# Sixteen-wavelength attention: part of the exponentials computed by exponent splitting and a polynomial on VectorE

## The chip, the cores and the metric

The kernel runs on one core of a Trainium2 chip. The time is device microseconds of that core for one execution of the whole program; lower is better. Engines are named as in the profile: PE (TensorE) does matmuls and transposes, ACT (ScalarE) activation functions, DVE (VectorE) elementwise work and reductions, POOL (GpSimd) a few elementwise operations, SP (SyncE) issues DMAs.

## The reference

Six layers act in turn on a residual stream of 4 batches x 1024 tokens x 128 features: a mixture of experts, a state-space layer, the same mixture again, a second mixture, an attention layer, and that second mixture again. Only the attention is touched by the change:

```python
# B = 4, S = 1024, H = 16 heads, D = 8, 16 wavelengths (WL)
Q, K, V = proj(Wq, bq), proj(Wk, bk), proj(Wv, bv)
def wl_step(acc, wl):
    cpm, iw = wl
    m = cpm[None, :, None, None]
    scores = jnp.einsum('bhqd,bhkd->bhqk', Q * m, K * m) * SCALE
    scores = scores * jnp.cos(KERR * scores * scores)
    attn = jax.nn.softmax(scores, axis=-1)
    return (acc + jnp.einsum('bhqk,bhkd->bhqd', attn, V) * iw, None)
```

KERR is 2.7e-12, so for the drawn data the cosine is 1 and the kernel takes a branch (`attention_small`) that leaves it out. What is left is, for each of 64 (batch, head) pairs and 16 wavelengths, a softmax of one 1024 x 1024 score matrix scaled by a number c(head, wavelength), times the values. One (batch, head, wavelength) is called a channel here: 1024 channels, each with a million exponentials, 8192 in each of the 128 partitions.

## The kernel before

The layers run one after the other with the residual stream `x_sb` resident in SBUF. In the attention, the scores of a (batch, head) `u` are computed once, less each row's maximum, into `xs[u]` (128 key rows x 8 key tiles x 1024 queries), and the 16 channels of `u` share them.

The loop over channels (lines 798 to 850) does this for each `wl` of each `u`:

- ACT computes `p_w = exp(c * xs[u])` over all 8192 elements in one instruction (line 812). `p_w` has two buffers.
- PE multiplies it by the values `vts` (lines 821 to 827): 8 key tiles `i` x 4 query quarters `r`, which show as 64 matmul records. The value tile carries a column of ones, so that the same product gives the softmax's denominator. The results lie in one of two PSUM tiles `ob`, in turn.
- DVE copies the product to SBUF (`os`, line 829), PE transposes it (line 842), and in every second channel DVE copies the transposes of two channels into `ot` (line 846).

Beside the channel of the current head, work for later ones is spread over the channels, a piece in each, by Python generators:

- `prepare(u + 2)`, 16 pieces: first `maxima`, in which PE computes a score tile (line 712), DVE reduces it to row maxima `nm` (line 726), and the eighth piece also transposes the maxima on PE (line 734) and writes them into a row of `qp` (line 741); then `head`, in which PE computes a score tile and DVE copies it to `xs` (line 750).
- `group`, in four channels of every fourth head: projections (line 691) and their copies with bias (line 698).
- `batch`, five pieces for each next batch: layer norm, transposes and values.
- `out`, eight pieces for each finished batch: `project` transposes the combined heads (line 511), copies them (`ct`, line 513), multiplies (line 515) and adds to `x_sb` (lines 517 and 518).
- `weigh`, once for each head, in the first channel of the next one: four DVE operations (lines 757 to 770) divide by the denominators, weight and sum the 16 wavelengths into `comb`.

For PE and DVE the order in the queues is the order in which the program is written: the whole loop stands under `manual_schedule(engines={PE, DVE})`. ACT runs its exponentials in order. An engine takes its instructions in order and each waits for the data that it needs, so an instruction that waits holds up all that stand behind it on its engine.

Within a channel of before, PE's queue has: the `o` matmuls, the side piece's matmuls, the score matmuls, the transposes of `os`. DVE's has: the `os` copy, `weigh` if due, the side piece, the score copy or reduction, the `ot` copy.

Of the kernel before, what the change touches and what calls it, by code (L numbers as in the profile page):

```python
# [19 lines left out]
F32 = mybir.dt.float32  # L20
I32 = mybir.dt.int32
AF = mybir.ActivationFunctionType
ALU = mybir.AluOpType
# [3 lines left out]
P = 128  # L27
B, L, C = 4, 1024, 128
GT = L // P
# [8 lines left out]
H, D, WL = 16, 8, 16  # L38
# [4 lines left out]
ROUND = 1.5 * 2.0**23  # L43
PI2_1 = 6.28125
PI2_2 = 0.0019350051879882812
PI2_3 = 2.0 * math.pi - PI2_1 - PI2_2
RSQRT = 1597463007.0
LN_TINY = -87.33654

# [23 lines left out]
def ln_stats(nc, sb, x, mv, rstd):  # L73

    n = x.shape[1]
    for i in range(n):
# [7 lines left out]
    nc.vector.tensor_scalar(  # L84
        rstd.bitcast(I32), a.bitcast(I32), -0.5, RSQRT, op0=ALU.mult, op1=ALU.add
    )
# [383 lines left out]
def half_sine(nc, sb, t, n):  # L470
# [6 lines left out]
    nc.vector.scalar_tensor_tensor(r, kk, -PI2_2, r, op0=ALU.mult, op1=ALU.add)  # L477
    nc.vector.scalar_tensor_tensor(r, kk, -PI2_3, r, op0=ALU.mult, op1=ALU.add)
    nc.vector.tensor_scalar(r, r, 4.0, -4.0, op0=ALU.min, op1=ALU.max)
# [42 lines left out]
NG = H // HG  # L522
QQ = 4
QW = L // QQ


def attention(tc, k):
# [8 lines left out]
    with ExitStack() as ctx:  # L536
# [51 lines left out]
        with tc.If(small > 0) as cmp:  # L588
            attention_small(tc, k, cc, iw)
# [4 lines left out]
def attention_small(tc, k, cc, iw):  # L594
# [9 lines left out]
    nc = tc.nc  # L604
    with (
# [9 lines left out]
        for x, w_t in (("q", k.wq), ("k", k.wk)):  # L615
# [11 lines left out]
            for j in range(HG):  # L627
                nc.sync.dma_start(
                    out=b_t[32 * j + 1 : 32 * j + 1 + D, :],
# [4 lines left out]
        vts = []  # L634
        for j in range(2):
            vt = one.tile([P, GT, H, D + 1], F32, name=f"vt{j}")
            nc.gpsimd.memset(vt[:, :, :, D : D + 1], 1.0)
            vts.append(vt)
        ob = []
        for j in range(2):  # L640
            o = ps_o.tile([P, 512], F32, name=f"o{j}", tag=f"o{j}")
            nc.vector.memset(o[:, 0:QW], 0.0)
            ob.append(o)

        xnt, qp, kp, comb, xs = {}, {}, {}, {}, {}

        def batch(b):

            xnt[b] = sb.tile([P, L], F32, name="xnt", bufs=1)
            mv = sb.tile([P, GT, 2], F32, name="mv")  # L650
            rstd = sb.tile([P, GT], F32, name="rstd")
            ln_stats(nc, sb, k.x_sb[:, ts(b, GT), :], mv, rstd)
            yield
            for half in range(2):
                pt = ps_t.tile([P, 4, P], F32, name="pt", tag="tr")
                for i in range(4):
                    t = b * GT + half * 4 + i
                    xn = sb.tile([P, C], F32, name="ln_xn", bufs=4)
                    nc.vector.tensor_scalar(
                        xn,  # L660
                        k.x_sb[:, t, :],
                        mv[:, half * 4 + i, 0:1],
                        rstd[:, half * 4 + i : half * 4 + i + 1],
                        op0=ALU.subtract,
                        op1=ALU.mult,
                    )
                    nc.tensor.transpose(pt[:, i, :], xn, k.ident)
                nc.vector.tensor_copy(xnt[b][:, ts(half, 512)], pt.rearrange("p a b -> p (a b)"))
                yield
            for half in range(2):  # L670
                pv = ps_t.tile([P, 4, H, D], F32, name="pv", tag="tr")
                for i in range(4):
                    nc.tensor.matmul(
                        pv[:, i], xnt[b][:, ts(half * 4 + i, P)], k.wv, start=True, stop=True
                    )
                for i in range(4):
                    nc.vector.tensor_tensor(
                        vts[b % 2][:, half * 4 + i, :, 0:D],
                        pv[:, i],
                        k.bv.rearrange("p (h d) -> p h d", d=D),  # L680
                        op=ALU.add,
                    )
                yield

# [61 lines left out]
        def head(u):  # L746
            n, j = divmod(u, HG)
            xs[u] = xp.tile([P, GT, L], F32, name="xs")
            for i in range(GT):
                nc.vector.tensor_copy(xs[u][:, i, :], score(j, kp[n], i, qp[n]))  # L750
                yield

        def weigh(u, ot):

            b, h = divmod(u, H)
            rz = sb.tile([P, WL, 2 * QQ], F32, name="rz", bufs=1)
            nc.vector.reciprocal(rz, ot[:, :, :, D])
            nc.vector.tensor_tensor(
                rz, rz, iw[:, :, None].to_broadcast([P, WL, 2 * QQ]), op=ALU.mult
            )  # L760
            nc.vector.tensor_tensor(
                ot[:, :, :, 0:D],
                ot[:, :, :, 0:D],
                rz[:, :, :, None].to_broadcast([P, WL, 2 * QQ, D]),
                op=ALU.mult,
            )

            if h == 0:
                comb[b] = sb.tile([P, 2, QQ, C], F32, name="comb")
            nc.vector.tensor_reduce(  # L770
                comb[b].rearrange("p c r e -> p (c r) e")[:, :, ts(h, D)],
                ot[:, :, :, 0:D].rearrange("p w t d -> p t d w"),
                AX.X,
                ALU.add,
            )

        def out(b):
            for c in range(2):
                for r in range(QQ):
                    project(nc, k, sb, ps_t, "tr", b * GT + 2 * r + c, comb[b][:, c, r, :])  # L780
                    yield

        def finish(*pieces):
            for piece in pieces:
                for _ in piece:
                    pass

        def prepare(u):

            yield from maxima(u)  # L790
            yield from head(u)

        n_heads = B * H
        with tc.manual_schedule(engines={mybir.EngineType.PE, mybir.EngineType.DVE}):
            finish(batch(0), group(0), prepare(0))
            ahead = prepare(1)
            next(ahead)
            for u in range(n_heads):
                n, j = divmod(u, HG)
                b, h = divmod(u, H)  # L800

                beside = []
                if j == 2 and n + 1 < B * NG:
                    beside.append((10, 14, group(n + 1)))
                if n % NG == 3 and j == 1 and b + 1 < B:
                    beside.append((4, 9, batch(b + 1)))
                if b > 0 and h == 2:
                    beside.append((2, 10, out(b - 1)))
                ot = sb.tile([P, WL, 2 * QQ, D + 1], F32, name="ot", bufs=1)
                for wl in range(WL):  # L810
                    p_w = xp.tile([P, GT, L], F32, name="p_w")
                    nc.scalar.activation(  # L812
                        p_w.rearrange("p a b -> p (a b)"),
                        xs[u].rearrange("p a b -> p (a b)"),
                        AF.Exp,
                        scale=cc[:, h, wl : wl + 1],
                    )
                    o = ob[wl % 2]
                    for i in range(GT):
                        for r in range(QQ):  # L820
                            nc.tensor.matmul(  # L821
                                o[32 * r : 32 * r + D + 1, 0:QW],
                                vts[b % 2][:, i, h, :],
                                p_w[:, i, ts(r, QW)],
                                start=(i == 0),
                                stop=(i == GT - 1),
                            )
                    os = sb.tile([P, QW], F32, name="os")
                    nc.vector.tensor_copy(os, o[:, 0:QW])  # L829
                    if u > 0 and wl == 0:  # L830
                        weigh(u - 1, last)
                    for lo, hi, piece in beside:
                        if lo <= wl < hi:
                            next(piece)
                    if wl == WL - 1 and u + 2 < n_heads:
                        finish(ahead)
                        ahead = prepare(u + 2)
                    next(ahead, None)
                    if wl % 2 == 0:
                        pt = ps_t.tile([P, 4, P], F32, name="pt", tag="tr")  # L840
                    for c in range(2):
                        nc.tensor.transpose(  # L842
                            pt[:, wl % 2 * 2 + c, :], os[:, ts(c, P)], k.ident
                        )
                    if wl % 2 == 1:
                        nc.vector.tensor_copy(
                            ot[:, wl - 1 : wl + 1].rearrange("p w t d -> p (w t) d"),
                            pt.rearrange("p a (r e) -> p (a r) e", e=32)[:, :, 0 : D + 1],
                        )
                last = ot  # L850
            weigh(n_heads - 1, last)
            finish(out(B - 1))

# [250 lines left out]
```

## Time and profile before

| | |
|---|---|
| median of 3 runs | 8823.45 us (8822.91 to 8829.49) |
| the profiled execution | 8833.98 us, its span in the trace 8832.1 us |
| before the attention loop's first exponential | 1424.5 us of the span |
| attention's channels | 7237.1 us of the span |
| after it | 170.5 us of the span |
| busy, whole span: PE, PEld, DVE, ACT, POOL | 7823.0, 3392.0, 3262.1, 7665.0, 608.7 us |
| granted PE clock, whole span | 0.918 |

PEld are weight loads, which run beside the matmuls. A busy PE is not a PE at its peak, as ends of matmuls are modelled. A mean duration of an instruction includes its latency, so that independent instructions in a row overlap a little: the distance from start to start is what counts in a chain. POOL's 608.7 us all lie ahead of the attention loop.

### The profile page before, as it was taken

The page shows a single profiled execution, that of the slowest core. Times are in us where ns is not written, and L with a number is a line of the kernel's source. Part 1 is how long each engine was busy: PE and PEld are TensorE (multiplying, and loading weights), DVE is VectorE, ACT ScalarE, POOL GpSimd, SP SyncE. Part 2 cuts the span into 40 slices and gives each one's busy share as a digit, 9 for nine tenths or more (in the row PEclk, how much of TensorE's full clock was granted, in tenths as well). Part 3 has the DMA queues.
Part 4 walks back from the last instruction along what each step waited for, and adds up shares of the span by engine and source line. Part 5 has one row for each costly group of instructions (what it writes and reads, how often), then busy time and mean ns, then how long its engine had stood idle before and what let it go on. Part 6 is the DMA issues. An engine that isn't in the chain of part 4 may idle for free. (4 is left out here: it accounts for less than half of the span.)

```text
span 8832.1 us, 164134 instructions
## 1 busy us (share of the span) xinstructions
PE 7823.0 (89%) x76474; PEld 3392.0 (38%) x76474; DVE 3262.1 (37%) x5409; ACT 7665.0 (87%) x1746; POOL 608.7 (7%) x579
## 2 busy tenths in 40 slices
PE   8888887999899998989999999999999999899985
PEld 5222253333333333333333333333333333333333
DVE  6777773323333333323233323223333333323222
ACT  3333325999999999999999999999999999999992
POOL 3444430000000000000000000000000000000000
PEclk9777787999999999999999999999999999999996
DMA  0000000000000000000000000000000000000000
GB/s 18 0 0 0 0 6 4 1 1 1 1 1 1 1 1 1 1 1 1 1 1 1 1 1 1 1 1 1 1 1 1 1 1 1 1 1 1 1 1 16
DMA packets 14326, 19.40 MB, mean 2 GB/s; under 512 B 2986, under 2 KB 12722, under 8 KB 13620
## 3 DMA queue, kind: packets, MB, share of 16 engines
q8 instruction: 609, 9.98, 0.5%
q1 hardware_dynamic: 9316, 6.01, 0.2%
q10 hardware_dynamic: 4304, 2.62, 0.1%
q14 instruction: 97, 0.79, 0.0%
HBM read 6.53 MB, written 2.10 MB: 1 GB/s over the span
## 5 line engine op out<-in xcount | busy, mean ns | idle before, releaser
L812 ACT ACTIVATE p_w<-xs,cc 128x8192 f32<-128x8192 f32 x1024 | 7188.6, 7109 | 48.5 <-DVE xs L750 29.1
L821 PE MATMUL o<-p_w,vt 128*9 128x256 f32 x65536 | 4055.1, 403 | 654.3 <-ACT p_w L812 653.4
L821 PEld LDWEIGHTS o<-p_w,vt 128*9 128x9 f32 x65536 | 1809.4, 95 | 2608.2 <-ACT p_w L812 804.3
L829 DVE COPY os<-o 128x256 f32<-128x256 f32 x1024 | 434.9, 425 | 3595.2 <-PE o L821 3595.2
L712 PE MATMUL s<-kp,qp 32*128 32x512 f32 x2048 | 1026.5, 621 | 0.0
L712 PE MATMUL s<-qp,kp 32*128 32x512 f32 x2048 | 1022.1, 619 | 0.0
L750 DVE COPY xs<-s 128x1024 f32<-128x1024 f32 x512 | 627.1, 1225 | 730.4 <-PE s L712 724.3
L726 DVE TENSOR_REDUCE nm<-s 128x1 f32<-128x1024 f32 x512 | 626.2, 1223 | 647.5 <-PE s L712 647.5
L712 PEld LDWEIGHTS s<-qp,kp 32*128 32x128 f32 x2048 | 343.6, 186 | 491.2 <-issue 486.9
L712 PEld LDWEIGHTS s<-kp,qp 32*128 32x128 f32 x2048 | 344.7, 186 | 471.7 <-issue 467.0
L842 PEld LDWEIGHTS pt<-ident,os 128*128 128x128 f32 x2048 | 206.2, 141 | 764.1 <-issue 669.0
L354 PE MATMUL yp<-hm,ident 128*128 128x512 f32 x512 | 388.7, 880 | 99.2 <-POOL hm L353 97.7
L842 PE MATMUL pt<-ident,os 128*128 128x128 f32 x2048 | 450.3, 302 | 19.6 <-DVE os L829 9.6
L336 ACT ACTIVATE da<-delta,neg_a 128x512 f32<-128x512 f32 x256 | 182.7, 721 | 291.9 <-DVE hst L342 291.5
L353 POOL TENSOR_TENSOR hm<-hst,c_sb 128x512 f32<-128x512 f32 x256 | 369.9, 1457 | 166.3 <-ACT c_sb L333 113.3
L178 ACT ACTIVATE r<-hp 128x512 f32<-128x512 f32 x160 | 95.5, 597 | 207.9 <-PE hp L176 185.5
L354 PEld LDWEIGHTS yp<-hm,ident 128*128 128x128 f32 x512 | 110.0, 252 | 348.9 <-POOL hm L353 318.0
L340 DVE TENSOR_TENSOR db<-du,bp 128x512 f32<-128x512 f32 x256 | 164.2, 682 | 152.9 <-PE bp L329 152.0
L333 ACT COPY c_sb<-cp 128x512 f32<-128x512 f32 x128 | 74.8, 585 | 166.1 <-PE cp L331 129.0
L342 DVE TENSOR_TENSOR_SCAN hst<-da,last,db 128x512 f32<-128x512 f32 x128 | 192.0, 1540 | 0.0
L180 POOL TENSOR_TENSOR h<-r 128x512 f32<-128x512 f32 x160 | 164.6, 1047 | 201.7 <-ACT r L178 201.3
L342 DVE TENSOR_TENSOR_SCAN hst<-da,db 128x512 f32<-128x512 f32 x128 | 171.1, 1372 | 5.6 <-POOL hm L353 4.4
(176 smaller groups left out, 3102.8 us busy)
## 6 DMA issues: line engine op xcount, KB each, us to landing
x_sb<-in_L_attn_x_dram ACTq DMA_DIRECT2D x4, 512.0 KB
c_w<-in_L_ffn_w_dram SPq DMA_DIRECT2D x4, 512.0 KB
out_dram<-x_sb SPq DMA_DIRECT2D x4, 512.0 KB
c_w<-in_L_ffn_w_stack_dram SPq DMA_DIRECT2D x1, 512.0 KB
c_w<-in_L_ffn_w_stack_dram ACTq DMA_DIRECT2D x1, 512.0 KB
c_ws<-in_L_ffn_ws_dram SPq DMA_DIRECT2D x2, 128.0 KB
c_w_in<-in_L_attn_W_in_dram SPq DMA_DIRECT2D x1, 256.0 KB
c_w_out<-in_L_attn_W_out_dram SPq DMA_DIRECT2D x1, 128.0 KB
```

Source lines behind the costliest of these rows:

```text
L180: nc.gpsimd.tensor_tensor(h, r, r, op=ALU.mult)
L336: nc.scalar.activation(da, delta[:, c, hc], AF.Exp, scale=neg_a[:, c, n : n + 1])
L342: nc.vector.tensor_tensor_scan(hst, da, db, 0.0 if half == 0 else last[:, c, n : n + 1], op0=ALU.mult, op1=ALU.add,)
L353: nc.gpsimd.tensor_tensor(hm, hst, c_sb, op=ALU.mult)
L354: nc.tensor.matmul(yp[c], k.ident, hm, start=(n == 0), stop=(n == NS - 1))
L712: nc.tensor.matmul(s[:, ts(half, 512)], a[row, ts(i, P)], c[row, ts(half, 512)], start=True, stop=True,)
L726: nc.vector.tensor_reduce(nm[:, i : i + 1], score(j, qp[n], i, kp[n]), AX.X, ALU.max, negate=True)
L750: nc.vector.tensor_copy(xs[u][:, i, :], score(j, kp[n], i, qp[n]))
L812: nc.scalar.activation(p_w.rearrange("p a b -> p (a b)"), xs[u].rearrange("p a b -> p (a b)"), AF.Exp, scale=cc[:, h, wl : wl + 1],)
L821: nc.tensor.matmul(o[32 * r : 32 * r + D + 1, 0:QW], vts[b % 2][:, i, h, :], p_w[:, i, ts(r, QW)], start=(i == 0), stop=(i == GT - 1),)
L829: nc.vector.tensor_copy(os, o[:, 0:QW])
L842: nc.tensor.transpose(pt[:, wl % 2 * 2 + c, :], os[:, ts(c, P)], k.ident)
```

## The change

512 of the 8192 exponentials of each channel (`SOFT = 512`: key tile 0 with the first 512 queries) are no longer computed by ACT. With log2(e) folded into the scale (`cc2`), DVE computes r = max(c x, -127), rounds it to a whole number p (adding and subtracting a large constant), and makes the bits of 2^p as an integer e; POOL subtracts, r = r - p; and DVE evaluates a polynomial of fifth degree in r by four nested steps and a last one that multiplies by 2^p and writes `p_w`. The polynomial's leading coefficient is left out of it and multiplied into a copy of the values, `vtops`, which PE uses for these two of the 32 products of a channel.

The channels are numbered through, g = 16 u + wl. In channel g, right behind the `os` copy, DVE does `power(g + 1)`, the five polynomial steps; behind the score copy it does `split(g + 2)`, the three operations ahead of POOL's subtraction, which `power(g + 2)` will use in the next channel. ACT's instruction now covers 7680 elements and the matmuls of a channel are as many as before.

Smaller edits make room in SBUF: `ln_xn` has two buffers in place of four, `comb` one in place of two, `out` of a finished batch runs in head 0, channels 1 to 8, in place of head 2, channels 2 to 9. The scratch tiles of the new operations have one buffer each.

```diff
+SOFT = 512
...
+        vtops = [one.tile([P, H, D + 1], F32, name=f"vtop{j}") for j in range(2)]
+        cc2 = one.tile([P, H, WL], F32, name="cc2")
+        nc.vector.tensor_scalar(cc2, cc, LOG2E, None, op0=ALU.mult)
...
-                    xn = sb.tile([P, C], F32, name="ln_xn", bufs=4)
+                    xn = sb.tile([P, C], F32, name="ln_xn")
...
+                if half == 0:
+                    nc.vector.tensor_scalar(
+                        vtops[b % 2], vts[b % 2][:, 0], EXP2_TOP, None, op0=ALU.mult
+                    )
...
+        def split(g):
+            u, wl = divmod(g, WL)
+            s, c = xs[u][:, 0, 0:SOFT], cc2[:, u % H, wl : wl + 1]
+            r = sb.tile([P, SOFT], F32, name="x_r", bufs=1)
+            nc.vector.tensor_scalar(r, s, c, -127.0, op0=ALU.mult, op1=ALU.max)
+            p = sb.tile([P, SOFT], F32, name="x_p", bufs=1)
+            nc.vector.tensor_scalar(p, r, ROUND, ROUND, op0=ALU.add, op1=ALU.subtract)
+            e = sb.tile([P, SOFT], I32, name="x_e", bufs=1)
+            nc.vector.tensor_scalar(
+                e, p, float(1 << 23), 127.0 * (1 << 23), op0=ALU.mult, op1=ALU.add
+            )
+            nc.gpsimd.tensor_tensor(r, r, p, op=ALU.subtract)
+            return e, r, p
+
+        def power(g, e, r, p):
+            p_w[g] = xp.tile([P, GT, L], F32, name="p_w")
+            nc.vector.scalar_tensor_tensor(p, r, EXP2[4], r, op0=ALU.add, op1=ALU.mult)
+            for c in EXP2[3], EXP2[2], EXP2[1]:
+                nc.vector.scalar_tensor_tensor(p, p, c, r, op0=ALU.add, op1=ALU.mult)
+            nc.vector.scalar_tensor_tensor(
+                p_w[g][:, 0, 0:SOFT], p, EXP2[0], e.bitcast(F32), op0=ALU.add, op1=ALU.mult
+            )
...
-                comb[b] = sb.tile([P, 2, QQ, C], F32, name="comb")
+                comb[b] = sb.tile([P, 2, QQ, C], F32, name="comb", bufs=1)
...
+            power(0, *split(0))
+            parts = split(1)
             for u in range(n_heads):
...
-                if b > 0 and h == 2:
-                    beside.append((2, 10, out(b - 1)))
+                if b > 0 and h == 0:
+                    beside.append((1, 9, out(b - 1)))
...
-                    p_w = xp.tile([P, GT, L], F32, name="p_w")
+                    g = u * WL + wl
                     nc.scalar.activation(
-                        p_w.rearrange("p a b -> p (a b)"),
-                        xs[u].rearrange("p a b -> p (a b)"),
+                        p_w[g].rearrange("p a b -> p (a b)")[:, SOFT:],
+                        xs[u].rearrange("p a b -> p (a b)")[:, SOFT:],
                         AF.Exp,
                         scale=cc[:, h, wl : wl + 1],
                     )
...
+                            soft = i * L + r * QW < SOFT
                             nc.tensor.matmul(
                                 o[32 * r : 32 * r + D + 1, 0:QW],
-                                vts[b % 2][:, i, h, :],
-                                p_w[:, i, ts(r, QW)],
+                                vtops[b % 2][:, h, :] if soft else vts[b % 2][:, i, h, :],
+                                p_w[g][:, i, ts(r, QW)],
                                 start=(i == 0),
                                 stop=(i == GT - 1),
                             )
                     os = sb.tile([P, QW], F32, name="os")
                     nc.vector.tensor_copy(os, o[:, 0:QW])
+                    if g + 1 < n_heads * WL:
+                        power(g + 1, *parts)
                     if u > 0 and wl == 0:
                         weigh(u - 1, last)
...
                     next(ahead, None)
+                    if g + 2 < n_heads * WL:
+                        parts = split(g + 2)
```

## The prediction

> **What bounds the kernel now.** I read the page's costliest groups first, then the sums over three stretches (before, in and after the attention loop), then the timeline of plain channels, then the sums over single stretches of 3.41 us. A "channel" is one pass of the `wl` loop, 1024 in all.
>
> ```profile
> L812 ACT ACTIVATE p_w<-xs,cc 128x8192 f32<-128x8192 f32 x1024 | 7188.6, 7109 | 48.5 <-DVE xs L750 29.1
> L829 DVE COPY os<-o 128x256 f32<-128x256 f32 x1024 | 434.9, 425 | 3595.2 <-PE o L821 3595.2
> 1424.50:8661.60 7237.10, 6545.55 (x72820) 2800.15 (x72821) 2226.43 (x3187) 7188.57 (x1025) 0.00 (x0) 0.95 0.01 1
> ```
>
> The third line is the stretch of attention: elapsed time, then busy time of PE, PEld, DVE, ACT and POOL, then the granted clock. ACT is busy 7188.6 of 7237.1 us: the exponential paces attention at 7237.1/1024 = 7.07 us a channel. POOL does nothing there, DVE works 31% of it. Everything else is 8832.1 - 7237.1 = 1595 us, which the change leaves alone.
>
> ```profile
> 5016.03 3.64 PE L821 MATMUL o<-p_w,vt 128*9 128x256 f32 x64
> 5019.60 1.98 PE L712 MATMUL s<-qp,kp 32*128 32x512 f32 x4
> 5019.74 0.42 DVE L829 COPY os<-o 128x256 f32<-128x256 f32 x1 [2.74 <-PE o L821]
> 5021.51 0.44 PE L842 MATMUL pt<-ident,os 128*128 128x128 f32 x2
> 5021.62 1.22 DVE L750 COPY xs<-s 128x1024 f32<-128x1024 f32 x1 [1.46 <-PE s L712]
> 5022.71 3.64 PE L821 MATMUL o<-p_w,vt 128*9 128x256 f32 x64 [0.76 <-ACT p_w L812]
> ```
>
> One channel on PE and DVE (start, length, engine, operation). The 64 `o` matmuls start at 5016.03; `os` can be copied 3.71 us later. PE itself could repeat every 3.57 + 1.91 + 0.37 = 5.85 us; it waits for ACT. What matters below: between two `o` blocks DVE owes PE nothing but the short `os` copy.
>
> **What the Trainium skill says.** "VectorE: DVE Perf Modes", section "Mode 2×_2P — use both read ports for one tensor": fp32 operations with one tensor source in SBUF take two elements a cycle, those with two tensor sources one. The trace agrees: at 128x1024, `tensor_scalar` L313 took 0.69 us, `scalar_tensor_tensor` L314 and L316 1.23 us. The five polynomial steps have two tensor sources.
>
> ```profile
> 221.28 0.69 DVE L313 TENSOR_SCALAR sp_w<-sp_z 128x1024 f32<-128x1024 f32 x1 [1.14 <-ACT sp_z L311]
> 222.01 1.23 DVE L314 SCALAR_TENSOR_TENSOR sp_z<-sp_w,sp_z 128x1024 f32<-128x1024 f32 x1
> 223.27 1.23 DVE L316 SCALAR_TENSOR_TENSOR sp_v<-sp_v,sp_z 128x1024 f32<-128x1024 f32 x1
> ```
>
> "SBUF — State Buffer", section "🔬 SBUF: two separate sides": VectorE (two-port mode or two SBUF inputs) and GpSimd take one port pair as an exclusive lock. Here L353 on POOL shows 1.26 and 2.24 us for one shape.
>
> "TensorE: Matmul & The Clock Gate", section "What's actually happening": a free-running window of about 3.4 us with too little matmul work is followed by half clock. The trace agrees, one line for each such stretch (elapsed, PE and PEld busy with `o` matmuls alone and their counts, clock):
>
> ```profile
> 5001.54:5004.96 3.42, 3.12 (x60) 1.66 (x64) 1.00 0.02 5
> 5004.96:5008.37 3.41, 0.52 (x12) 0.02 (x3) 1.00 0.00 0
> 5008.37:5011.78 3.41, 3.10 (x32) 1.22 (x36) 0.50 0.00 0
> 5011.78:5015.20 3.42, 2.04 (x40) 0.72 (x30) 1.00 0.00 0
> ```
>
> Only 12 `o` matmuls in the second stretch, so half clock in the third: that block took 5.14 us in place of 3.64.
>
> **The change part by part.**
>
> *ACT.* Successive exponentials start 7.02 us apart ((70.28 - 7.11)/9 over ten of them) for 8192 elements, 7680 cost 512/8192 of the streaming part less: at most 0.44 us, so about 6.59. As the only effect this would give 8832 - 0.43 x 1024 = 8392. It isn't, because ACT stops being last.
>
> *The chain that appears.* The built program holds DVE in this order: `os` copy of channel g, the five steps of `power(g+1)`, `weigh` or side work, the score copy, the three of `split(g+2)`, the `ot` copy. The `os` copy waits for the last `o` matmul of g; the first `o` matmul of g+1 reads the part that `power(g+1)` writes, and PE works in order. So PE and DVE alternate. The period, from one `o` start to the next:
> - 3.71 us to the `os` copy (timeline above);
> - 0.34 until the next DVE instruction starts (in the timeline `os` at 5054.53, then the reciprocal at 5054.87);
> - five steps at 128x512 with two tensors. L197, same operation and shape, takes 0.69 us; each step reads the previous result, and such a pair in the timeline (L314, L316) leaves about 0.03 between end and start: 4 x 0.725 + 0.69 = 3.59;
> - about 0.10 for two semaphore waits (21 ns each) and the hand-over to PE (`os` end to `pt` start is 0.06 in the last head).
>
> Sum 7.74 us. It covers PE's scores and transposes (they end at 5.85) and ACT's 6.59: ACT is a whole channel ahead. 1024 x 7.74 = 7926.
>
> *Under the `o` block.* DVE then does the score copy (1.14 to the next start), `split` (a pointer scale; L313's 0.69 at 1024 leaves about 0.42 at 512, L268's pointer adds 0.06: 0.48 + 0.42 + 0.42 with gaps, 1.38) and half an `ot` copy (0.15): 2.7 us of the 3.7. Hidden; without that cover it would cost 1.4 us. POOL's subtraction (1.04 by L180, 1.26 by L353) starts at about 2.2 and must be done by 4.05: hidden by 0.5 to 0.8 us, and if the port lock makes it 2.24, 0.4 us late. I take 0, keep 0 to 0.4. The whole part's integer output could lose two-port mode (+0.27): hidden.
>
> *Work that DVE now delays.* `weigh`, 63 times between channels: 0.94, 0.29, 1.23, 2.08 us, 4.57 to the next start. It pushes the score copy, `split` and POOL, which end about 7.9 to 8.3 after the `o` start, not before 4.05: +3.8, 239 us. The last maximum of each of 62 heads: PE's row-maximum transposes wait for a reduction that now stands behind `power`; from that reduction to the next `o` the trace has 5100.17 to 5102.53, 2.36 us, and it starts 0.14 before that `o` would otherwise: +2.2, 136 us. `out`, 24 pieces: PE waits for `ct` behind `power`, then scores (1.91) and transposes (0.37) follow: +2.8, 67 us; moving it from h = 2 to h = 0 changes nothing. `batch`, three times: statistics and transposes with half the `ln_xn` buffers, about 12 us each (statistics 8 x (0.28 + 0.16) + 15 small ones of 0.2 = 6.5, less 1.3 of slack, and two transposing pieces at 3.5), 36. `group`'s 0.75 us copies fit in the slack: 0. `comb` with one buffer: the next batch's first `weigh` writes it a whole head after `out`'s last piece has read it: 0. `vtop`, `cc2`: 0. Sum 478.
>
> *Clock.* The quiet part (no `o` matmul) grows from 7.02 - 3.57 = 3.45 to 7.74 - 3.57 = 4.17 us. A window is too quiet when it holds less than about 0.7 us of `o` (12 matmuls at 0.057): chances per channel (3.45 + 0.7 - 3.41)/3.41 = 0.22 before, (4.17 + 0.7 - 3.41)/3.41 = 0.43 after. Before, the page's 4055.1/1024 = 3.96 us against 3.64 agrees: 0.32 lost of 1.5. Then ACT's wait hid most; now the `o` block is on the path. A full-clock and a half-clock period together, 7.74 + 9.24 = 16.98 us, are nearly five windows, so it may lock at every second channel: 0.43 to 0.5 times 1.5, I take 0.70 us a channel, 717 us; bounds 0.28 and 1.0.
>
> *Sum.* 1595 + 7926 + 478 + 717 = 10716 us of span. The profiled execution itself took 8833.98 for 8832.1 of span, and the median of the runs shown is 8823.45, 10.5 lower: 10716 + 1.9 - 10.5, about 10707.
>
> **The rivals.**
> - *The clock holds.* PE's chain is as above but quiet windows cost only what they do now (0.28): 10716 - 430 = 10286, median about 10277. For it: the window count is a fit to one kernel. Against: the gap plainly grows.
> - *The dependent steps overlap.* DVE starts independent 512-wide operations every 0.60 us (db pair in 1.28); if dependent ones did too, five take 3.09: 7.24 a period, 10716 - 512 = 10204 before any clock gain, near 10000 with it. Against: L314 to L316.
> - *Not slower: the polynomial runs at two elements a cycle.* A step then starts every 0.45 us (0.42 + 0.03). The whole balances at 1024 x (period + 0.28) + 478 = 7237, a period of 6.32, so five steps in 2.2 us: 0.445 each. Below that point the chain is shorter than ACT's and ACT's saving counts; with 6.59 a channel and half of the extras, 1595 + 6748 + 240 = 8583, median about 8570. Against it: L197 and L316 show one element a cycle in this very operation.
>
> **How the numbers follow.** Main case 0.72; clock holds 0.16; overlap 0.07; not slower 0.05. The main case's own range, 10450 to 11050, comes from the clock's bounds (-430, +307) and POOL's lateness. With the first two rivals: 10100 to 11100. The measurement tells 0.2% from no change. Slower 0.95, same 0.01, faster 0.04.
>
> **What would show it.** `o` blocks waiting on DVE's final `p_w` step, not on ACT; `os` starts about 8.4 to 8.9 us apart on average; ACT busy about 6.75 ms and idle over 2 ms on PE or DVE; polynomial rows near 690 ns; a granted clock below 0.95 in attention; POOL finishing before `os`. It is wrong if `p_w`'s steps show below 0.5 us, if ACT stays back to back, or if POOL is what the first step waits for in plain channels.

## The result

The change makes the kernel slower: 11107.43 us median (11099.07 to 11116.91, 4 runs) against 8823.18 us, a ratio of 1.259 (95% interval 1.2568 to 1.2612). The forecast was 10707 us, with a range of 10100 to 11100: the direction and the chain of PE and DVE were right, the size was 400 us short, and the time lies 7 us above the range.

The page of the kernel after, its engine sums and costliest groups (busy and mean ns of one, then idle time just before them and what ended it):

```profile
PE 8657.6 (78%) x76474; PEld 3629.8 (33%) x76474; DVE 7900.4 (71%) x13606; ACT 7321.7 (66%) x1746; POOL 2093.1 (19%) x1603
...
L859 ACT ACTIVATE p_w<-xs,cc 128x7680 f32<-128x7680 f32 x1024 | 6845.4, 6697 | 2649.3 <-PE o L869 2186.3
L869 PE MATMUL o<-p_w,vt 128*9 128x256 f32 x61440 | 4774.6, 459 | 0.0
...
L788 DVE SCALAR_TENSOR_TENSOR x_p<-x_p,x_r 128x512 f32<-128x512 f32 x3072 | 2125.7, 692 | 105.1
L869 PE MATMUL o<-p_w,vtop 128*9 128x256 f32 x4096 | 704.0, 425 | 1824.3 <-DVE p_w L789 1824.3
L877 DVE COPY os<-o 128x256 f32<-128x256 f32 x1024 | 434.4, 424 | 2155.4 <-PE o L869 2155.4
```

ACT saved 343 us of work (7188.6 to 6845.4) and now idles 2649 us, mostly for `o`. The two long waits face each other: the `o` block waits 1824 us for DVE's last polynomial step, DVE's `os` copy waits 2155 us for the `o` block. Two engines that wait for each other in turn are a chain, and neither is full. The mean `o` matmul with `vt` went from 403 to 459 ns.

The timeline of two plain channels after (start, length, engine, operation, idle before):

```profile
5009.68 0.39 PE L869 MATMUL o<-p_w,vtop 128*9 128x256 f32 x2 [1.85 <-DVE p_w L789]
5009.69 0.39 PE L869 MATMUL o<-p_w,vt 128*9 128x256 f32 x2
5009.90 0.39 PE L869 MATMUL o<-p_w,vtop 128*9 128x256 f32 x2
5009.91 5.09 PE L869 MATMUL o<-p_w,vt 128*9 128x256 f32 x58
...
5014.94 1.98 PE L726 MATMUL s<-kp,qp 32*128 32x512 f32 x4
5015.08 0.42 DVE L877 COPY os<-o 128x256 f32<-128x256 f32 x1 [3.00 <-PE o L869]
...
5015.42 0.68 DVE L786 SCALAR_TENSOR_TENSOR x_p<-x_r 128x512 f32<-128x512 f32 x1
5016.13 2.15 DVE L788 SCALAR_TENSOR_TENSOR x_p<-x_p,x_r 128x512 f32<-128x512 f32 x3
5016.85 0.44 PE L894 MATMUL pt<-ident,os 128*128 128x128 f32 x2
5018.38 0.69 DVE L789 SCALAR_TENSOR_TENSOR p_w<-x_p,x_e 128x512 f32<-128x512 f32 x1
...
5019.13 0.39 PE L869 MATMUL o<-p_w,vtop 128*9 128x256 f32 x2 [1.84 <-DVE p_w L789]
...
5022.84 0.42 DVE L877 COPY os<-o 128x256 f32<-128x256 f32 x1 [1.09 <-PE o L869]
...
5026.89 0.39 PE L869 MATMUL o<-p_w,vtop 128*9 128x256 f32 x2 [1.84 <-DVE p_w L789]
```

The second channel runs from 5019.13 to 5026.89: 7.76 us, where 7.74 had been forecast. The first has the same chain but its `o` block at half clock: 5009.68 to 5019.13, 9.45 us, 1.69 more. A plain channel is one with no side work and no last maximum of a head, and not directly behind `weigh`: 807 of them, of which 60% are of the slow kind, counted in the trace. The sums over the attention loop say the same in the last but two column, the granted clock, which was 0.95 before:

```profile
1428.50:10923.20 9494.70, 7382.69 (x72780) 3043.04 (x72784) 6868.23 (x11376) 6845.40 (x1025) 1483.81 (x1024) 0.87 0.00 1
```

### The profile page after: what moved, and what is told of

Its sections match the earlier page's. It is cut to its first block, busy times and chain, and to the rows that moved or that the text cites. A ratio compares the mean times of both kernels' runs of the same rounds, so it can differ in the third digit from the quotient of the medians.

```text
span 11097.3 us, 175440 instructions
## 1 busy us (share of the span) xinstructions
PE 8657.6 (78%) x76474; PEld 3629.8 (33%) x76474; DVE 7900.4 (71%) x13606; ACT 7321.7 (66%) x1746; POOL 2093.1 (19%) x1603
## 5 line engine op out<-in xcount | busy, mean ns | idle before, releaser
L859 ACT ACTIVATE p_w<-xs,cc 128x7680 f32<-128x7680 f32 x1024 | 6845.4, 6697 | 2649.3 <-PE o L869 2186.3
L869 PE MATMUL o<-p_w,vt 128*9 128x256 f32 x61440 | 4774.6, 459 | 0.0
L780 POOL TENSOR_TENSOR x_r<-x_r,x_p 128x512 f32<-128x512 f32 x1024 | 1483.8, 1449 | 8078.8 <-DVE x_p L775 8078.8
L788 DVE SCALAR_TENSOR_TENSOR x_p<-x_p,x_r 128x512 f32<-128x512 f32 x3072 | 2125.7, 692 | 105.1
L869 PE MATMUL o<-p_w,vtop 128*9 128x256 f32 x4096 | 704.0, 425 | 1824.3 <-DVE p_w L789 1824.3
L789 DVE SCALAR_TENSOR_TENSOR p_w<-x_p,x_e 128x512 f32<-128x512 f32 x1024 | 708.8, 692 | 109.4 <-DVE x_p L788 4.1
L786 DVE SCALAR_TENSOR_TENSOR x_p<-x_r 128x512 f32<-128x512 f32 x1024 | 699.0, 683 | 59.5 <-POOL x_r L780 56.8
L773 DVE TENSOR_SCALAR x_r<-xs,cc 128x512 f32<-128x512 f32 x1024 | 489.0, 478 | 1.6
L777 DVE TENSOR_SCALAR x_e<-x_p 128x512 int32<-128x512 f32 x1024 | 437.6, 427 | 35.3
L775 DVE TENSOR_SCALAR x_p<-x_r 128x512 f32<-128x512 f32 x1024 | 437.6, 427 | 35.3
```

The lines of the kernel that those rows point to most:

```text
L773: nc.vector.tensor_scalar(r, s, c, -127.0, op0=ALU.mult, op1=ALU.max)
L775: nc.vector.tensor_scalar(p, r, ROUND, ROUND, op0=ALU.add, op1=ALU.subtract)
L780: nc.gpsimd.tensor_tensor(r, r, p, op=ALU.subtract)
L786: nc.vector.scalar_tensor_tensor(p, r, EXP2[4], r, op0=ALU.add, op1=ALU.mult)
L788: nc.vector.scalar_tensor_tensor(p, p, c, r, op0=ALU.add, op1=ALU.mult)
L789: nc.vector.scalar_tensor_tensor(p_w[g][:, 0, 0:SOFT], p, EXP2[0], e.bitcast(F32), op0=ALU.add, op1=ALU.mult,)
```

## The experiments

Each ran beside the kernel before. "Slow" channels are those whose 64 `o` matmuls take over 4.2 us from the first start to the last, 3.26 at full clock; counted in the traces.

### Matmuls in PE's gap: eight, then four

```diff
+FILL = 8
...
+                    if FILL:
+                        for f in range(FILL):
+                            nc.tensor.matmul(
+                                ob[(wl + 1) % 2][:, 256 + f % 2 * 128 : 384 + f % 2 * 128],
+                                k.wo,
+                                k.wo,
+                                start=True,
+                                stop=True,
+                            )
                     if wl % 2 == 1:
                         nc.vector.tensor_copy(
```

The second kernel has `FILL = 4`.

> Eight 128x128 matmuls of constant data are added to each channel behind the transposes of os, written to the unused half of the other o bank; nothing reads them. Eight at about 0.22 us fill the 1.84 us in which PE waits for the polynomial. Theory (the shortfall of the forecast is the clock: 60% of the channels have their o block at half speed, 1.69 us each, because windows with too little matmul work are followed by half clock): the slow share falls under 0.2, the plain period stays 7.76 to 7.9, the time falls from 11107 to 10200 to 10500. Rival (the slow blocks have another cause, such as the DVE or POOL traffic beside them): the slow share stays near 0.6 and the time stays or rises.

> Four instead of eight of e1's added matmuls in each channel, 0.9 of PE's 1.84 us of waiting. Theory of the clock: between, nearer to e1 if what counts is that quiet windows rise above a threshold: slow share 0.05 to 0.4, 10400 to 10800. Rival (the gain of e1 came from something else that eight matmuls change, such as the place of the o block): no reduction of the slow share in plain channels.

Measured: with eight 10448.78 us (ratio 1.1837, 1.1817 to 1.1857), with four 10413.37 us (1.1789, 1.1771 to 1.1807), so 659 and 694 us less than the change although PE has more to do. The timeline with eight (they show as 16 records):

```profile
5004.05 1.95 PE L900 MATMUL o<-c_wo 128*128 128x128 f32 x16
5005.31 0.69 DVE L790 SCALAR_TENSOR_TENSOR p_w<-x_p,x_e 128x512 f32<-128x512 f32 x1
...
5006.05 0.39 PE L870 MATMUL o<-p_w,vtop 128*9 128x256 f32 x2
```

The added work ends as the polynomial does, and `o` follows without the wait of 1.84 us; the plain period stays 7.76 us (median). Slow shares of the plain channels: 0.60 with none, 0.09 with four, 0.02 with eight. What plain channels lose beyond 7.76 us falls from 857 us to 154 and 44. Four give a better time than eight since the eight lie open where PE had no gap to spare: behind the last maximum of a head a channel loses 4.3 us with eight, 3.3 with four, and a `group` channel takes 8.7 us against 7.9. The DVE and POOL work beside the `o` blocks is the same in all three, so it isn't what makes them slow: PE's own quiet is. How much of the shortfall this explains is worked out below.

### The polynomial one channel earlier

```diff
                     nc.vector.tensor_copy(os, o[:, 0:QW])
-                    if g + 1 < n_heads * WL:
-                        power(g + 1, *parts)
+                    if g + 2 < n_heads * WL:
+                        parts = split(g + 2)
...
                     next(ahead, None)
                     if g + 2 < n_heads * WL:
-                        parts = split(g + 2)
+                        power(g + 2, *parts)
```

Ahead of the loop, `power(1, *split(1))` joins `power(0, *split(0))`. The same instructions run; `power(g + 2)` may write its `p_w` buffer as soon as `o` of channel g has read it, which the `os` copy has waited for anyway.

> Same work; only the places in DVE's queue change: split(g+2) directly behind the os copy of g, power(g+2) as the last thing of channel g, so no o block waits for a polynomial that was begun after the o block before it. Theory (the position between os and the next o block is what costs): DVE's own load becomes the bound, about 7.1 us a channel, 8850 to 9100 in all. Rival (the added DVE work costs the same wherever it stands): above 10500.

Measured: 9061.37 us, ratio 1.0263 (1.0246 to 1.028). The place alone is worth 2046 us of the 2284. The group of `o` matmuls that waits for a polynomial nearly vanishes as a wait (1824.3 us of idle time in the change):

```profile
L869 PE MATMUL o<-p_w,vtop 128*9 128x256 f32 x4096 | 673.8, 410 | 7.4 <-DVE p_w L789 7.4
```

In the attention DVE, the third of the busy times, now works 92% of the time, and in plain channels it runs from one `os` copy to the next without idle time:

```profile
1428.00:8885.00 7457.00, 6694.70 (x72759) 2813.80 (x72757) 6878.09 (x11372) 6772.80 (x1024) 1488.82 (x1023) 0.93 0.01 1
5002.29 0.41 DVE L877 COPY os<-o 128x256 f32<-128x256 f32 x1
...
5008.80 0.42 DVE L877 COPY os<-o 128x256 f32<-128x256 f32 x1
```

That is 6.51 us, less than the 7.02 between exponentials before. By the periods in the two traces, channels without side work, `weigh` or a last maximum in or just ahead of them are some 320 us faster in all than in the kernel before. What makes the kernel slower all the same are the channels in which DVE has more to do: some 350 us are lost in and behind those with `weigh`, 100 in those with `out`, 50 with `batch` and 40 with the last maximum.

### Only the last polynomial step

```diff
-            nc.vector.scalar_tensor_tensor(p, r, EXP2[4], r, op0=ALU.add, op1=ALU.mult)
-            for c in EXP2[3], EXP2[2], EXP2[1]:
-                nc.vector.scalar_tensor_tensor(p, p, c, r, op0=ALU.add, op1=ALU.mult)
             nc.vector.scalar_tensor_tensor(
-                p_w[g][:, 0, 0:SOFT], p, EXP2[0], e.bitcast(F32), op0=ALU.add, op1=ALU.mult
+                p_w[g][:, 0, 0:SOFT], r, EXP2[0], e.bitcast(F32), op0=ALU.add, op1=ALU.mult
             )
```

> Leaves out the first four of the five polynomial steps of each channel (the outputs are not those of the reference). Theory (chain of os copy, five steps, o block): four steps of 0.725 us go from the chain, 7.76 becomes 4.86, below ACT's 6.61 a channel; time 8450 to 8750. Rival (the chain is not what sets the period but, say, POOL's subtraction or ACT's waiting): above 9500.

Measured: 8496.56 us, ratio 0.9623 (0.9607 to 0.9639). With the chain 2.9 us shorter ACT paces again, nearly full in the 6899 us of the attention:

```profile
L856 ACT ACTIVATE p_w<-xs,cc 128x7680 f32<-128x7680 f32 x1024 | 6759.7, 6688 | 144.9 <-PE o L866 103.2
```

So ACT's saving is real (some 330 us) once DVE's chain is out of the way. `split` and POOL's subtraction are still there: with all else they leave ACT 144.9 us of idle time, 48.5 in the kernel before, so they cost little.

### Half the width in the order of the change

`SOFT = 256`, nothing else.

> SOFT = 256 with the order of the change: half the polynomial. Each step takes about 0.46 us from start to start (0.27 + 0.16 + 0.03), so the chain is 3.71 + 0.34 + 2.27 + 0.1 = 6.4 us, below ACT's 6.8. Theory: near ACT's bound, with some half-clock blocks on top, 8950 to 9400. Rival (a fixed cost of each added instruction dominates, whatever its width): above 9800.

Measured: 9222.36 us, ratio 1.0444 (1.0423 to 1.0466). The steps take 0.42 us and the plain channels at full clock come every 6.43 us where 6.4 was expected; 28% are slow and then take 8.12. The slow blocks eat what the shorter chain would win: on average a plain channel takes 7.01 us, 6.96 in the kernel before. Of the 390 us that the attention loses against before, only some 40 lie there; 165 lie behind `weigh`, 140 in channels with `out`, which the order of the change still delays.

### Half the width, one channel earlier

Both edits together, and in a second kernel `weigh` as a generator with one of its four operations in each of a head's first four channels (`ot` with two buffers, `out` four channels later).

> SOFT = 256 and the order of e2 (split right behind os, power two channels ahead as the last of the channel). Theory: ACT bounds again, at about 6.8 us a channel (7.02 less 256/8192 of the streaming part), since DVE's load is some 5.5 us and no o block waits for a fresh polynomial; weigh, maxima and out cost some 100 us: 8600 to 8760, faster than the kernel before the change. Rival (DVE's share of work delays the score copies enough to eat the 0.21 us a channel): 8823 or more.

> e5 with the four DVE operations of weigh spread over the first four channels of a head (ot with two buffers, out four channels later). Theory: takes back most of what weigh's 4.6 us block delays, 30 to 100 us below e5. Rival (that block is hidden by the two p_w buffers anyway): within 20 us of e5.

Measured: 8694.2 us, ratio 0.9855 (0.984 to 0.987), and 8694.79 us, ratio 0.9848 (0.9835 to 0.9862). The first is a version that beats both kernels, by 1.5% over the one before: a small gain, but clear of the interval. ACT is the bound again and nearly full:

```profile
L859 ACT ACTIVATE p_w<-xs,cc 128x7936 f32<-128x7936 f32 x1024 | 6974.8, 6898 | 130.6 <-PE o L869 98.4
L869 PE MATMUL o<-p_w,vt 128*9 128x256 f32 x63488 | 3786.1, 384 | 272.5 <-ACT p_w L859 270.3
1428.00:8517.00 7089.00, 6671.72 (x72741) 2792.24 (x72737) 5162.20 (x11363) 6958.39 (x1023) 787.05 (x1022) 0.99 0.01 1
```

ACT's work fell by 214 us against before (7188.6 to 6974.8) and its idle time rose by 82 (48.5 to 130.6); the difference is the gain. Spreading `weigh` brought nothing, as the rival expected: ACT's idle time, 122.9 us with it, was hardly touched. That the two `p_w` buffers hide the block, the rival's reason, fits this but wasn't shown by itself.

### The output projection behind the scores

```diff
                     for lo, hi, piece in beside:
-                        if lo <= wl < hi:
+                        if lo <= wl < hi and lo != 1:
                             next(piece)
...
                     next(ahead, None)
+                    for lo, hi, piece in beside:
+                        if lo <= wl < hi and lo == 1:
+                            next(piece)
```

> The change with the 24 pieces of out moved behind the score matmuls on PE (and behind the score copy on DVE). Theory (the 7.3 us that such a channel loses are PE's wait for ct, 2.8 us, and then the scores and transposes at half clock behind that empty wait): the scores run at full clock before the wait, the channel loses 3 to 5 us, 50 to 110 us less in all, 10990 to 11060. Rival (the project matmuls and copies themselves cost it): no difference beyond 20 us.

Measured: 11050.44 us, ratio 1.2516 (1.2497 to 1.2536), 57 us under the change, intervals apart. The change itself, one piece of `out`:

```profile
3810.96 0.80 PE L520 MATMUL po<-c_wo,ct 128*128 128x128 f32 x2 [4.07 <-DVE ct L518]
3811.69 3.78 PE L726 MATMUL s<-kp,qp 32*128 32x512 f32 x4
...
3815.40 0.69 PE L894 MATMUL pt<-ident,os 128*128 128x128 f32 x2
```

PE idles 4.07 us for `ct`, which DVE does behind `power`; everything after it, scores (3.78 for 1.98) and transposes (0.69 for 0.44), runs at half clock. In the experiment the scores stand ahead of the wait:

```profile
3806.16 1.98 PE L726 MATMUL s<-kp,qp 32*128 32x512 f32 x4
...
3811.69 0.79 PE L520 MATMUL po<-c_wo,ct 128*128 128x128 f32 x2 [3.29 <-DVE ct L518]
```

Such a channel now loses 4.4 us, before 7.3 (24 of them, 70 us; more slow blocks elsewhere took some 14 back). The edit takes the scores off the path behind `ct` altogether and puts DVE's reduction, 1.1 us to the next start, ahead of `ct`. With scores at full clock, 1.9 us, that would win about 0.8 us a channel (an estimate from these lines); at half clock, where they took 3.7, about 2.6. It won 2.9, so most of the gain is the half clock's.

## Where the prediction was right, and which steps failed

The attention took 9494.7 us of the span; the forecast had 9121. Its terms, from the periods between `o` blocks in the trace of after (channels put to one row each; "clock" is what the `o` block takes above 3.26 us, not counted behind `weigh`, where it is hidden):

| term | forecast, us | measured, us |
|---|---|---|
| the chain, 7.74 us a channel | 7926 | 7938 (7.76) |
| `weigh` | 239 | 242 (60 x 4.03) |
| last maximum of a head (57; six more fall under `out` and `batch`) | 136 | 128 |
| `out` | 67 | 143 |
| `batch` | 36 | 58 |
| `o` blocks at half clock | 717 | 978 |
| other plain and `group` channels | 0 | 9 |
| sum | 9121 | 9496 |

The other 25 of the 400 us lie outside: the rest of the program took 1602.6 us in place of 1595, and the median came out 10.1 us above the profiled span, where 8.6 below it had been carried over.

- **The chain: right.** 3.71 us to `os`, five steps of 0.69 with 0.03 between, nothing overlapped; PE's scores and ACT lie under it. The last-step and the one-channel-earlier kernels show that it set the period. The rival of overlapping steps and that of two elements a cycle fell: the steps measured 683 and 692 ns.
- **Under the `o` block: right.** `split` took 0.48 + 0.43 + 0.43; the integer output kept the speed of the others. POOL's subtraction took 1.45 us, more than the 1.04 to 1.26 taken, but was waited for only 56.8 us in all, 49 of them in the channels behind `weigh`.
- **`weigh` and the maxima: right** to 3 and 8 us.
- **The clock: the failed step.** The forecast took 0.70 us a channel, 717 us, from the rule "a window is too quiet when it holds less than about 0.7 us of `o`"; measured were 978 us. The rule counted `o` alone and was read from one window, in which scores filled most of the rest: PE was busy 2.80 of 3.41 us there. In the change PE is idle for 1.84 us of a plain period, and windows with more `o` work are still too quiet. Two such windows of after, each with the one behind it (elapsed, busy time and count of `o` matmuls and of their weight loads, clock):

```profile
4064.78:4068.19 3.41, 1.05 (x20) 0.56 (x24) 1.00 0.00 0
4068.19:4071.60 3.41, 3.41 (x37) 1.42 (x32) 0.50 0.02 5
4081.84:4085.26 3.42, 0.91 (x20) 0.49 (x24) 1.00 0.00 0
4085.26:4088.67 3.41, 3.41 (x40) 1.39 (x36) 0.50 0.00 0
```

  20 matmuls, not 12, with PE busy 1.57 us in all, and half clock follows. Both traces can be sorted window by window (full clock in the window, what follows it; the clock changes only in steps of 3.413 us). In the kernel before, half clock followed 139 of 189 windows with less than 0.7 us of `o`, and 59 windows with more: the share came out right because 50 and 59 errors cancelled. In the change it followed 391 of 435, and 222 with more. So the rule was wrong in the kernel before already, and there it didn't show. A larger limit on `o` isn't the answer: the forecast's formula with 1.2 us gives 0.57 for the change, where 0.60 of the plain channels are slow, but 0.36 for the kernel before, where 0.19 of all are.

  One count fits both kernels: PE's busy time without the scores, and a fifth of the scores' (a score matmul uses 32 rows of weights, the others 128). Below 1.55 us of 3.41, half clock followed 195 of 208 windows before and 602 of 613 after; above, 3 of 1685 and 11 of 1437. The fifth and the 1.55 are fitted, and ends of matmuls are modelled; with the same two numbers none of 2407 windows is wrong with eight added matmuls, 5 of 2341 with four, and 52 of 1871 with the polynomial one channel earlier at full width. By this count a window with a channel's scores and transposes has about 0.8 us from them and needs 0.7 of `o`, the forecast's figure; one that begins behind the scores, with the 1.84 us of idle time in it, needs 1.1.

  A slow block also cost 1.69 us, not 1.5. The forecast of 0.70 us a plain channel was 1.06 (854/807), over all channels 978/1023 = 0.96, just inside the bound of 1.0 that the range used; with `out` and `batch` on top the time left the range. The "clock holds" rival fell. The Trainium skill's page "TensorE: Matmul & The Clock Gate" (section "🎯 Why this matters for your kernels") warns of idle gaps of more than about 3 us; here 1.84 us in every period was enough. Both experiments with added matmuls show that it is PE's quiet that costs this. The term was 261 us short, the larger part of the 400.
- **`out`: the second miss, in the main of the same cause.** It was 76 us short, 6.0 us a piece in place of 2.8 (7.3 with the slow `o` blocks of these channels, which the table counts under the clock). The wait for `ct` was counted, but not that the scores and transposes behind it run at half clock, which is 2.1 of the 3.2 us by the lines above. The rest, and the 22 us of `batch`, no experiment took apart; nor were the smaller buffers and the new place of `out` tried alone.
- **The range** did not follow from its own terms: the clock's lower bound, -430, gives 10277 and not 10450, and its upper one with POOL's full 0.4 us a channel gives about 11420 and not 11050. So the range's end, 7 us under the measured time, has little weight; the terms above say where the forecast failed.

## What to carry to other kernels

Moving work off a full engine helps only if the receiving engine's instructions stand where nobody waits for them: here the same added DVE instructions cost 2284 us with the polynomial between the `os` copy and the next matmul block, and 235 us (9061.37 against 8826.69 beside it) with it one channel earlier. When a change makes PE wait, price the wait twice, for itself and for the half-clock stretch behind it, and check a rule for that on every window of a trace, with all kinds of matmuls in it, before it is carried over: a share that comes out right can hide errors that cancel. Choose the share that moves by the receiver's load: 256 of 8192 gained 1.5%, 512 lost 2.6% in the same order.

## What the runs showed of the hardware

- A gap of only 1.84 us of idle PE in a 7.76 us period kept 60% of the matmul blocks at half clock. Four 128x128 matmuls in it, about 1 us, brought that to 9% and the whole kernel 694 us down.
- In the kernel that beats both, the granted clock in the attention was 0.99, against 0.95 before: there the first `o` matmuls of a plain channel no longer wait for ACT, and PE waits 272 us for ACT in all, 654 before. That this is why was not tested.
- What came ahead of half clock was not a gap of a certain length but a window of 3.413 us with little work, in which 32-row score matmuls weigh about a fifth of the others: one limit, 1.55 us of such work, sorts 3905 of the 3943 full-clock windows of the two kernels' attention.
- POOL's subtraction of two 128x512 tensors took 1.45 us in the attention, and its product of two, L353, 1.27 (median) ahead of it. Whether DVE's work beside it makes the difference was not tested.
